# Four selective-scan layers: transfers in program order, delta's second half by transfer, softplus in one piece per chunk, another layout of the layer norm

## The chip, the cores and the metric

The kernel runs on one core of a Trainium2 chip. The metric is device time of one execution in microseconds (us), the median of several runs. A profile comes from one more execution, whose own time and span are given beside it. Engines are called as in the profile: PE (matrix multiplications; PEld its weight loads), DVE (vector), ACT (activation), POOL (GpSimd) and SP, which here only issues transfers (DMAs).

## What is computed

Eight images of 64 x 64 positions with 96 channels go through four layers one after the other, each `x = x + f(groupnorm(x))`. Cut to what matters, `f` is a projection, a depthwise convolution with SiLU, and selective scans over the 4096 positions for 192 channels of 16 states, in four directions (layers 0 to 2) or one (layer 3):

```python
x_dbl = einsum('bkdl,kcd->bkcl', xs, x_proj_w)          # xs: 4 orders of the positions
dts, Bs, Cs = split(x_dbl, [rank, rank + 16])
delta = softplus(einsum('bkrl,kdr->bkdl', dts, dt_proj_w) + dt_bias)
def step(h, inp):                                       # over the positions
    u_t, d_t, b_t, c_t = inp
    h = exp(d_t[..., None] * A) * h + (d_t * u_t)[..., None] * b_t[:, :, None, :]
    return h, einsum('bkdn,bkn->bkd', h, c_t)
y = sum of the directions + D * xs, put back in order
y = layernorm(y) * gamma + beta                         # over 192 channels; layers 0 to 2
return (y * silu(z)) @ out_proj_w.T
```

## The kernel before, in words

A hardware loop runs over the eight images; its body holds the four layers. All data is fp32.

*Chunks.* A layer walks through its directions in the order k = 0, 2, 1, 3, eight chunks of 512 positions each: 32 chunks for layers 0 to 2, 8 for layer 3, 104 per image. k = 0 and 1 run forward, k = 2 and 3 backward. The projection of a forward chunk (`project`, `keep_x_dbl`) gives the rows of its backward partner too; these go to memory (`xm`) and are read back later by `load_x_dbl`.

*Partitions.* 192 channels are three groups t of 64. A tile of 128 partitions holds one group for two states at a time (the halves of the partitions), so a chunk is 24 scans of 128 x 512 (`scan`, L872): 6 steps s (two halves of the states g, three groups t) of four.

*What a scan needs.* Its decay is `exp(delta * A)` from ACT (`decay`, L858), with delta's 64 channels in both halves of the partitions. Its input, delta times u times B, comes from PE in PSUM (`enter`, L841, tile dbu: 16 matmuls of 64 x 64 for two scans); they take `du_t` (positions on partitions) and diagonal matrices built from B (`diagonal` on POOL for the first half of the states, `diagonals` on ACT for the second). After four scans POOL multiplies by C (`read_out`, L890), and PE adds the states up (`add_up`, L904).

*How delta comes about.* PE turns x_dbl into positions on partitions and applies the weights (`turn_v`, L716: four blocks of 128 positions, which are every fourth one), ACT works out softplus in three steps (Abs, Exp, Ln), DVE finishes it (`delta_of`, L752), PE turns u (`turn_u`, L730) and DVE multiplies (`du_of`, L763), PE turns delta back (`turn_back`, L815) and ACT copies it out of PSUM (`keep_delta`, L820 and L824).

*Order.* Between `tc.manual_schedule` and `by_hand.close()` PE, DVE, ACT and POOL run in program order; SP's transfers are placed by the scheduler. Inside the scans the order is written out: a chunk has 24 slots, one per scan. At slot m an `enter` goes out for two scans ahead (even slots), the scan, a decay four scans ahead, an `add_up` (odd slots), and what `plan` holds for the slot, which prepares the next chunk. In the plan before, chunk i + 1 is prepared in two halves e of two blocks each: `turn_v` at slots 2, 3 and 9, 10, softplus at 4 to 6 and 11 to 13, `delta_of` at 8 and 16, `du_of` at 12 and 18, `turn_back` at 17, 18, 20, 21, `keep_delta` at 19, 20 and 23, `project` for the chunk after at 22 and 23, copied out at slot 1. `spread_c` loads C in two parts, each spread over the partitions.

*PSUM.* `ps_b` holds two tiles of two banks (dbu and the wide ones), `ps_y` two single banks, `ps_m` two single banks, which x_dbl, v, u_t, delta_ps and the convolution's sums use in turn.

*Ahead of the scans* stands the convolution (partly on PE, DVE, ACT with POOL), during which the layer's first chunk is prepared without the plan, and `by_columns` writes a transposed copy of u to memory. *Behind them*, in the scheduler's order, come layer norm and gate: for a pair of chunks PE centres y by matmuls with a centring matrix (ca for channels 0 to 127, two banks; cb for 128 to 191 of both chunks), ACT squares, PE averages over the channels into all 128 partitions (var, L535 and L537), ACT makes Ln and Exp, DVE multiplies (L542, L543).

Of the kernel before, what the change touches and what calls it, by code (L numbers as in the profile page):

```python
# [30 lines left out]
DI = 192  # L31
# [11 lines left out]
NEGMEAN, CEN_A, CEN_B, ONE, EPS, N_CONST = 416, 544, 672, 736, 737, 738  # L43
# [73 lines left out]
def kernel(ctx: ExitStack, tc: tile.TileContext, x_in, const_in, *rest):  # L117
# [3 lines left out]
    def pool(name, bufs, space=None):  # L121
# [19 lines left out]
        ps_m=pool("ps_m", 2, PSUM),  # L141
# [23 lines left out]
def layer(tc, env, x, x_of, x_to, n, ly):  # L165
# [5 lines left out]
    mean_w = const[:, MEAN : MEAN + 128]  # L171
# [3 lines left out]
    def mm(name):  # L175
        return env.ps_m.tile([128, CH], F32, tag="mm", name=name)
# [41 lines left out]
    by_hand.enter_context(tc.manual_schedule(engines={E.PE, E.DVE, E.Activation, E.Pool}))  # L218
# [3 lines left out]
    m_ps = mm("m_ps")  # L222
# [7 lines left out]
    v_ps = mm("v_ps")  # L230
    nc.tensor.matmul(v_ps[0:C, 0:1], groups, var, start=True, stop=True)
    scale = small.tile([C, 1], F32, name="scale")
    with tables(tc, "natural_log_exp_and_others"):
        nc.scalar.activation(scale, v_ps[0:C, 0:1], AF.Ln, bias=const[0:C, EPS : EPS + 1])
        nc.scalar.activation(scale, scale, AF.Exp, scale=-0.5)
        n_a = K * NT * NJ
        neg_a = env.wts.tile([128, 4 * NT * NJ], F32, tag="neg_a", name=f"neg_a{n}")[:, :n_a]
        nc.scalar.activation(neg_a, w[:, ly.a_log : ly.a_log + n_a], AF.Exp)
        nc.vector.tensor_scalar(neg_a, neg_a, -1.0, None, ALU.mult)
# [66 lines left out]
    def by_taps(half, both, first=0, end=ly.taps):  # L306

        d0, nd = widths[half]
        if first == 0:
            sums[half, both[0]] = mm("conv")  # L310
# [46 lines left out]
    def make_ys():  # L357
# [3 lines left out]
        tc, env, n, ly, w, u_mem, lambda half: u_chunk(half, 0), d, neg_a, make_ys, mm, wide  # L361
    )
    early = next(work)
    if not image:
        early_at = {2: early.project, 3: early.turn, 5: early.turn_back, 6: early.keep_delta}
        with tables(tc, "silu_and_others"):
# [9 lines left out]
        with tables(tc, "natural_log_exp_and_others"):  # L376
            early.softplus()
        with tables(tc, "silu_and_others"):
# [9 lines left out]
    else:  # L388
# [69 lines left out]
        with tables(tc, "silu_and_others"):  # L458
# [27 lines left out]
        with tables(tc, "natural_log_exp_and_others"):  # L486
            early.softplus(lambda: by_vector(0, 3, 0))
        with tables(tc, "silu_and_others"):
# [16 lines left out]
    with tables(tc, "natural_log_exp_and_others"):  # L505
        ys = next(work)
    by_hand.close()
    y_a, y_b = ys
    x = load_x(tc, env, x_of)
# [6 lines left out]
    if ly.norm:  # L516
        with tables(tc, "natural_log_exp_and_others"):
            neg, cen_a = const[:, NEGMEAN : NEGMEAN + 128], const[:, CEN_A : CEN_A + 128]
            cen_b = const[:, CEN_B : CEN_B + 64]
            for c in range(0, NCH, 2):  # L520
                pair = chunks[c : c + 2]
                ca, cb = wide("ca").rearrange("p (o l) -> p o l", o=2), mm("cb")
                for o, s in enumerate(pair):
                    nc.tensor.matmul(ca[:, o], cen_a, y_a[:, s], start=True, stop=False)  # L524
                    nc.tensor.matmul(ca[:, o], neg, y_b[:, s], start=False, stop=True)
                for first, weights, y in ((True, neg[:, 0:64], y_a), (False, cen_b, y_b)):
                    for s, at in zip(pair, halves):
                        nc.tensor.matmul(cb[at], weights, y[:, s], start=first, stop=not first)  # L528
                sq_b = piece("sq_b")
                nc.scalar.activation(sq_b, cb, AF.Square)  # L530
                var = [single(o, "var") for o in range(2)]
                for o in range(2):
                    sq_a = piece("sq_a")
                    nc.scalar.activation(sq_a, ca[:, o], AF.Square)
                    nc.tensor.matmul(var[o], mean_w, sq_a, start=True, stop=False)  # L535
                for o, at in enumerate(halves):
                    nc.tensor.matmul(var[o], mean_w[at], sq_b[at], start=False, stop=True)  # L537
                for o, (s, at) in enumerate(zip(pair, halves)):
                    rstd = piece("rstd")
                    nc.scalar.activation(rstd, var[o], AF.Ln, bias=const[:, EPS : EPS + 1])  # L540
                    nc.scalar.activation(rstd, rstd, AF.Exp, scale=-0.5)
                    nc.vector.tensor_tensor(y_a[:, s], ca[:, o], rstd, ALU.mult)  # L542
                    nc.vector.tensor_tensor(y_b[at, pair[0]], cb[at], rstd[at], ALU.mult)  # L543


    with tables(tc, "silu_and_others"):
        for c in range(0, NCH, 2):
            pair = chunks[c : c + 2]
            z_a, z_b = wide("z_a").rearrange("p (o l) -> p o l", o=2), mm("z_b")
# [11 lines left out]
            if not ly.norm:  # L561
                of_b = mm("whole")
# [37 lines left out]
def scans(tc, env, n, ly, w, u_mem, u_first, d, neg_a, make_ys, mm, wide):  # L600
# [13 lines left out]
    RS, SL = 6, 24  # L614

# [20 lines left out]
    banks = {}  # L636

    def bank(i, name, part=0):

        if i > 0:  # L640
            return mm(name)
        if part == 0:
            banks[name] = wide(name)
        return banks[name][:, part * CH : part * CH + CH]
# [14 lines left out]
    def project(i, half):  # L659
# [3 lines left out]
        if half == 0:  # L663
            dbls[i] = bank(i, "x_dbl")[0 : ly.x_rows]
# [5 lines left out]
    def keep_x_dbl(i):  # L670
# [7 lines left out]
        nc.scalar.activation(x_dbl, dbls[i], AF.Identity, bias=const[0 : ly.x_rows, ONE : ONE + 1])  # L678
        nc.sync.dma_start(c_mem[k][:, s], x_dbl[0:NS])
        if K > 1:  # L680
            nc.sync.dma_start(x_mem[k + 2][:, s], x_dbl[64 : 64 + XP])
        dbls[i] = x_dbl[0:XP]

    def load_x_dbl(i):
# [5 lines left out]
        x_dbl = small.tile([128, CH], F32, tag="x_dbl", name="x_dbl")[0:XP]  # L690
        nc.sync.dma_start(x_dbl, x_mem[k][:, c * CH : (c + 1) * CH])
        dbls[i] = x_dbl
# [14 lines left out]
    def turn_v(i, e, b):  # L707

        if e == 0 and b == 0:
            for name in ("delta_t", "du_t"):  # L710
                turned[i, name] = env.turned.tile([128, NB4, DI], F32, tag=name, name=name)
        if b == 0:
            v = bank(i, "v", e)[:, 0 : 2 * (DI + NS)]
            turned[i, e, "v"] = v.rearrange("p (b d) -> p b d", b=2)
        at = ly.dt_w + walk[i][0] * (DI + NS)
        nc.tensor.matmul(  # L716
            turned[i, e, "v"][:, b],
            block(2 * e + b, dbls[i]),
            w[0:XP, at : at + DI + NS],
            start=True,  # L720
            stop=True,
        )

    def turn_u(i, e, b):

        if b == 0:
            to = bank(i, "u_t", e)[:, 0 : 2 * DI]
            turned[i, e, "u"] = to.rearrange("p (b d) -> p b d", b=2)
        to, b_ = turned[i, e, "u"], 2 * e + b
        nc.tensor.transpose(to[:, b, 0:128], block(b_, u_of(i, 0)), ident)  # L730
        nc.tensor.transpose(to[:, b, 128:DI], block(b_, u_of(i, 1)), ident[0:64, 0:64])  # L731

    def softplus(i, e, part):

        v = turned[i, e, "v"]
        if part == 0:
            rests[i, e] = env.turned.tile([128, 2, DI], F32, tag="rest", name="rest")
            nc.scalar.activation(rests[i, e], v[:, :, 0:DI], AF.Abs)
        elif part == 1:
            nc.scalar.activation(rests[i, e], rests[i, e], AF.Exp, scale=-1.0)  # L740
        else:
            nc.scalar.activation(rests[i, e], rests[i, e], AF.Ln, bias=1.0)

    def keep_b(i, e):

        bt = small.tile([128, 2, NS], F32, tag="bt", name="bt", bufs=4)
        nc.scalar.copy(bt, turned[i, e, "v"][:, :, DI:])  # L747
        turned[i, e, "b"] = bt

    def delta_of(i, e):  # L750

        nc.vector.scalar_tensor_tensor(  # L752
            turned[i, "delta_t"][:, 2 * e : 2 * e + 2],
            turned[i, e, "v"][:, :, 0:DI],
            0.0,
            rests.pop((i, e)),
            ALU.max,
            ALU.add,
        )

    def du_of(i, e):
        here = slice(2 * e, 2 * e + 2)
        nc.vector.tensor_tensor(  # L763
            turned[i, "du_t"][:, here], turned[i, "delta_t"][:, here], turned[i, e, "u"], ALU.mult
        )

    def diagonal(i, b):


        if b == 0:  # L770
            diags[i, 0] = env.diags.tile([128, NB4, NH, 64, 2], F32, tag="diag", name="diag")
        of = turned[i, b // 2, "b"][:, b % 2, 0:NJ].rearrange("p (q j) -> p q j", j=2)
        nc.gpsimd.tensor_tensor(  # L773
            diags[i, 0][:, b],
            sel.unsqueeze(1).unsqueeze(3).to_broadcast([128, NH, 64, 2]),
            of.unsqueeze(2).to_broadcast([128, NH, 64, 2]),
# [3 lines left out]
    def diagonals(i, first, n_):  # L780

        if first == 0:
            diags[i, 1] = env.diags.tile([128, NB4, NH, 64, 2], F32, tag="diag", name="diag")
        for q in range(first, first + n_):
            b, q = divmod(q, NJ)
            nc.scalar.activation(  # L786
                diags[i, 1][:, b, q // 2, :, q % 2],
                sel,
                AF.Copy,
                scale=turned[i, b // 2, "b"][:, b % 2, NJ + q : NJ + q + 1],  # L790
            )

    def diagonals_of_first():

        diags[0, 1] = env.diags.tile([128, NB4, NH, 64, 2], F32, tag="diag", name="diag")
        for b in range(NB4):
            of = turned[0, b // 2, "v"][:, b % 2, DI + NJ :].rearrange("p (q j) -> p q j", j=2)
# [7 lines left out]
    def turn_back(i, o, part):  # L805


        if part == 0:
            deltas[i, "ps", o] = bank(i, "delta_ps", o)
        for b in (2 * part, 2 * part + 1):  # L810
            of = turned[i, "delta_t"][:, b]
            for half in range(o + 1):
                to = deltas[i, "ps", o][64 * half : 64 * half + 128 // (o + 1)]
# [3 lines left out]
    def keep_delta(i, t):  # L817
        delta = env.deltas.tile([128, CH], F32, tag="delta", name="delta")
        if t == 2:
            nc.scalar.copy(delta, deltas[i, "ps", 1])  # L820
        else:
            for half in range(2):
                of = deltas[i, "ps", 0][64 * t : 64 * t + 64]
# [89 lines left out]
    def close_sums(i, o):  # L913
# [24 lines left out]
        2: [(turn_v, 1, 0, 0)],  # L938
        3: [(turn_v, 1, 0, 1)],
        4: [(keep_b, 1, 0), (softplus, 1, 0, 0)],  # L940
        5: [(softplus, 1, 0, 1)],
        6: [(softplus, 1, 0, 2), (diagonal, 1, 0), (turn_u, 1, 0, 0), (spread_c, 1, 0)],
# [194 lines left out]
```

## Time and profile before

| what | us |
| --- | --- |
| median of 3 runs (31732.65 to 31753.77) | 31743.75 |
| the profiled execution, its time | 31703.4 |
| its span | 31698.6 |
| PE busy in it | 30814.0 (97%) |
| DVE busy | 28392.2 (90%) |
| POOL busy | 27178.5 (86%) |
| ACT busy | 26085.1 (82%) |

Busy time is the union of an engine's instructions. The ends of matmuls are modelled, so PE's share says that it had work queued rather than that it ran at its peak. A line of the profile names the line of the code, the engine, the operation and the tiles, out<-in, with the sizes; a matmul in fp32 shows as two MATMUL records, its two passes. Windows cut out of the span show which engine fills a stretch; a timeline shows each engine's instructions in order, with the idle time ahead of one and what ended it in brackets. The granted clock of PE is 1.00 in the scans, and 0.98 over the span.

### The profile page before, as it was taken

To read this page: it belongs to the slowest core of one execution; us is meant where nothing else is said; L and a number is where in the kernel's file an instruction comes from. 1 tells how busy PE (TensorE), PEld (TensorE's weight loads), DVE (VectorE), ACT (ScalarE), POOL (GpSimd) and SP (SyncE) were. 2 spreads that over 40 slices of the span, in tenths; PEclk is the share of its full clock that TensorE was granted. 3 is DMA by queue.
4 is the path that set the end of the run, shared out by engine and by line. 5 is a ranking of instruction groups with operands and counts; after the bars stand their busy time and mean duration, and the time that the engine had idled before them with its cause. 6 is when DMAs were issued, how large, how long until landed. Compare 5 with 4: busy or idle time off the path is not lost. (4 is left out here: it accounts for less than half of the span.)

```text
span 31698.6 us, 951914 instructions
## 1 busy us (share of the span) xinstructions
PE 30814.0 (97%) x402320; PEld 16776.3 (53%) x402320; DVE 28392.2 (90%) x29432; ACT 26085.1 (82%) x65064; POOL 27178.5 (86%) x9436
## 2 busy tenths in 40 slices
PE   9999999999999999999999999999999999999999
PEld 5555555555555545555455554555555555555555
DVE  9899898998989989899898998989989899898998
ACT  8788788887888878888788887878878888788887
POOL 8898788987889879898798987989878898788987
PEclk9999999999999999999999999999999999999999
DMA  3333233333333333333333333333323333333332
GB/s 90 78 76 85 72 90 79 75 86 73 89 80 74 87 72 88 80 74 87 73 88 80 74 87 74 87 79 74 87 72 89 80 74 86 72 90 79 75 86 72
DMA packets 1262156, 2544.89 MB, mean 80 GB/s; under 512 B 108560, under 2 KB 129296, under 8 KB 1234832
## 3 DMA queue, kind: packets, MB, share of 16 engines
q1 hardware_dynamic: 1257872, 2483.64, 33.3%
q8 instruction: 3192, 52.30, 0.7%
q14 instruction: 1092, 8.95, 0.1%
HBM read 2208.74 MB, written 274.46 MB: 78 GB/s over the span
## 5 line engine op out<-in xcount | busy, mean ns | idle before, releaser
L890 POOL TENSOR_TENSOR h<-h,c 128x2048 f32<-128x2048 f32 x4992 | 22723.0, 4557 | 1867.5 <-ACT state L886 625.9
L872 DVE TENSOR_TENSOR_SCAN h<-d_a,state,dbu 128x512 f32<-128x512 f32 x17472 | 21076.5, 1261 | 1130.2 <-PE dbu L841 687.9
L858 ACT ACTIVATE d_a<-delta,neg_a 128x512 f32<-128x512 f32 x19968 | 14166.5, 716 | 122.1 <-DVE h L872 101.3
L841 PE MATMUL dbu<-diag,du_t 64*64 64x128 f32 x319488 | 11142.2, 277 | 296.4 <-DVE h L872 224.7
L841 PEld LDWEIGHTS dbu<-diag,du_t 64*64 64x64 f32 x319488 | 8712.0, 133 | 5111.5 <-issue 4681.5
L904 PE MATMUL y_ps<-h,const 128*64 128x512 f32 x39936 | 10827.0, 617 | 119.1 <-POOL h L890 110.5
L786 ACT ACTIVATE diag<-const,bt 128x64 f32<-128x64 f32 x25600 | 7550.4, 344 | 14.0 <-PE dbu L841 7.8
L773 POOL TENSOR_TENSOR diag<-const,bt 128x512 f32<-128x512 f32 x3328 | 3475.2, 1045 | 335.0 <-ACT bt L747 246.3
L872 DVE TENSOR_TENSOR_SCAN h<-d_a,dbu 128x512 f32<-128x512 f32 x2496 | 2881.8, 1203 | 498.6 <-ACT d_a L858 216.2
L904 PEld LDWEIGHTS y_ps<-h,const 128*64 128x64 f32 x39936 | 2065.6, 135 | 1899.4 <-issue 1498.5
L716 PE MATMUL v<-w,x_dbl 39*128 39x208 f32 (+1 forms) x6656 | 2618.4, 477 | 8.3 <-DVE delta_t L752 7.3
L716 PEld LDWEIGHTS v<-w,x_dbl 39*128 39x128 f32 (+1 forms) x6656 | 1787.2, 317 | 1568.3 <-issue 883.1
L824 ACT COPY delta<-delta_ps 64x512 f32<-64x512 f32 x3328 | 1930.9, 580 | 566.7 <-PE delta_ps L815 519.6
L815 PEld LDWEIGHTS delta_ps<-const,delta_t 128*64 128x64 f32 (+1 forms) x19968 | 1637.0, 154 | 1415.7 <-issue 949.7
L815 PE MATMUL delta_ps<-const,delta_t 128*64 128x128 f32 (+1 forms) x19968 | 2223.8, 286 | 11.6 <-issue 11.6
L747 ACT COPY bt<-v 128x32 f32<-128x32 f32 x1664 | 300.8, 183 | 1848.7 <-PE v L716 1846.5
L730 PEld LDWEIGHTS u_t<-const,u 128*128 128x128 f32 x3328 | 650.1, 195 | 1583.2 <-issue 887.2
L886 ACT COPY state<-h 128x4 f32<-128x4 f32 x4992 | 972.4, 195 | 568.0 <-DVE h L872 527.9
L454 POOL TENSOR_TENSOR acc<-acc,more 128x512 f32<-128x512 f32 x576 | 756.7, 1317 | 699.6 <-ACT more L453 356.1
L730 PE MATMUL u_t<-const,u 128*128 128x128 f32 x3328 | 1292.2, 388 | 0.0
L320 PE MATMUL conv<-xn,taps 96*128 96x512 f32 (+1 forms) x2496 | 1160.0, 658 | 22.1 <-DVE taps L203 22.1
L731 PE MATMUL u_t<-const,u 64*128 64x64 f32 x3328 | 1098.8, 330 | 0.0
(99 smaller groups left out, 16194.5 us busy)
## 6 DMA issues: line engine op xcount, KB each, us to landing
c<-cm SPq DMA_DIRECT2D x1792, 512.0 KB
c<-xm SPq DMA_DIRECT2D x1536, 512.0 KB
u<-u SPq DMA_DIRECT2D x1088, 256.0 KB
u<-u SPq DMA_DIRECT2D x1088, 128.0 KB
u<-u SPq DMA_DIRECT2D x48, 1024.0 KB
x_mem<-x SPq DMA_DIRECT2D x48, 768.0 KB
x<-x_mem SPq DMA_DIRECT2D x48, 768.0 KB
x<-in_x_dram SPq DMA_DIRECT2D x32, 768.0 KB
```

Source lines behind the costliest of these rows:

```text
L320: nc.tensor.matmul(part, taps[:, t, d0 : d0 + nd], rhs, start=t == 0, stop=t == ly.taps - 1)
L716: nc.tensor.matmul(turned[i, e, "v"][:, b], block(2 * e + b, dbls[i]), w[0:XP, at : at + DI + NS], start=True, stop=True,)
L730: nc.tensor.transpose(to[:, b, 0:128], block(b_, u_of(i, 0)), ident)
L773: nc.gpsimd.tensor_tensor(diags[i, 0][:, b], sel.unsqueeze(1).unsqueeze(3).to_broadcast([128, NH, 64, 2]), of.unsqueeze(2).to_broadcast([1 ...
L786: nc.scalar.activation(diags[i, 1][:, b, q // 2, :, q % 2], sel, AF.Copy, scale=turned[i, b // 2, "b"][:, b % 2, NJ + q : NJ + q + 1],)
L815: nc.tensor.matmul(block(b, to), of_, ident, start=True, stop=True)
L824: nc.scalar.copy(delta[64 * half : 64 * half + 64], of)
L841: nc.tensor.matmul(to[64 * half : 64 * half + 64, e, b], du[rows, b, 64 * t : 64 * t + 64], diag[rows, b, 2 * half + pair], start=True, st ...
L858: nc.scalar.activation(d_a, deltas[i, t], AF.Exp, scale=neg_a[:, at : at + 1])
L872: nc.vector.tensor_tensor_scan(hs[s][:, m4, flow], decays.pop(m)[:, flow], p[:, flow], 0.0 if first else states[i // NCH][:, j : j + 1], A ...
L890: nc.gpsimd.tensor_tensor(hs[s], hs[s], cs[i, g], ALU.mult)
L904: nc.tensor.matmul(sums[i][o][64 * half : 64 * half + 64], sel, hs[of][:, state, :], start=g == 0 and e in (0, 4), stop=g == 1 and e in (3 ...
```

## The change

1. SP joins the engines in program order (`E.SP` in `manual_schedule`); the table loads on ACT are then written plainly.
2. `ps_m` becomes one tile of two banks. x_dbl, v, delta_ps and u_t each take it whole, one after the other; outside the scans its halves are used by turns.
3. `turn_v` makes two blocks per call as a pair: one from x_dbl on partitions 0 up, one from a second copy on partitions 64 up, which a transfer makes (`x_hi`, or a second load of xm). The weights stand on both halves of the partitions.
4. Softplus, `keep_b`, `delta_of` and `du_of` are one instruction each per chunk, of 768 elements (64 for `keep_b`) per partition.
5. `turn_back` writes each group once; `keep_delta` copies 64 partitions out by ACT and fills the other 64 by a transfer.
6. The upper half of POOL's fourth diagonal goes to ACT (36 instead of 32 there).
7. The plan is written anew for this, with `turn_back` ahead of `turn_u`.
8. Layer norm: the mean and cb share a tile of two banks, both chunks side by side on the halves of the partitions; DVE subtracts the mean in place, in 64-partition pieces; var is one bank for both chunks; one Ln and four Exp of 64 partitions; POOL multiplies y_a, DVE y_b.

The first chunk of a layer goes the old way in points 3 and 5, with both copies from ACT and no transfer. Cut to the core:

```diff
-    by_hand.enter_context(tc.manual_schedule(engines={E.PE, E.DVE, E.Activation, E.Pool}))
+    by_hand.enter_context(tc.manual_schedule(engines={E.PE, E.DVE, E.Activation, E.Pool, E.SP}))
...
-        ps_m=pool("ps_m", 2, PSUM),
+        ps_m=pool("ps_m", 1, PSUM),
...
+    def two_banks(name):
+        return env.ps_m.tile([128, 2 * CH], F32, tag="mm", name=name)
...
                 pair = list(zip(chunks[c : c + 2], halves))
+                mean, cb = wide("mean").rearrange("p (o l) -> o p l", o=2)
+                for p, work in (
+                    (mean, ((mean_w, y_a), (mean_w, y_b))),
+                    (cb, ((neg, y_a), (cen_b, y_b))),
+                ):
+                    for last, (weights, y) in enumerate(work):
+                        for s, at in pair:
+                            nc.tensor.matmul(p[at], weights, y[:, s], start=not last, stop=bool(last))
+                var = single(c // 2 % 2, "var")
+                for s, at in pair:
+                    for half in halves:
+                        nc.vector.tensor_tensor(y_a[half, s], y_a[half, s], mean[at], ALU.subtract)
+                    sq_a = piece("sq_a")
+                    nc.scalar.activation(sq_a, y_a[:, s], AF.Square)
+                    nc.tensor.matmul(var[at], mean_w, sq_a, start=True, stop=False)
...
+                ln = env.decays.tile([128, CH], F32, tag="d_a", name="ln")
+                nc.scalar.activation(ln, var, AF.Ln, bias=const[:, EPS : EPS + 1])
+                for s, at in pair:
+                    rstd = env.decays.tile([128, CH], F32, tag="d_a", name="rstd")
+                    for half in halves:
+                        nc.scalar.activation(rstd[half], ln[at], AF.Exp, scale=-0.5)
+                    nc.gpsimd.tensor_tensor(y_a[:, s], y_a[:, s], rstd, ALU.mult)
+                    nc.vector.tensor_tensor(y_b[at, pair[0][0]], cb[at], rstd[at], ALU.mult)
...
 def keep_x_dbl(i):
+        dbls[i] = [x_dbl[0:XP], x_dbl[0:XP]]
+        if i > 0:
+            there = small.tile([128, CH], F32, tag="x_hi", name="x_hi", bufs=1)[64 : 64 + XP]
+            nc.sync.dma_start(there, x_dbl[0:XP])
+            dbls[i][1] = there
...
+    def turn_v(i, b):
+        for e, of in enumerate(dbls[i]):
+            o = 64 if i > 0 and e else 0
+            nc.tensor.matmul(
+                turned[i, "v"][:, 2 * e + b],
+                block(2 * e + b, of),
+                w[o : o + XP, at : at + DI + NS],
...
 def keep_delta(i, t):
+        if i > 0:
+            here = halves[t % 2]
+            nc.scalar.copy(delta[here], deltas[i, "ps"][here, t // 2])
+            nc.sync.dma_start(delta[halves[1 - t % 2]], delta[here])
...
     plan = {
         0: [(load_u, 2)],
         1: [(keep_x_dbl, 1)],
+        3: [(turn_v, 1, 0)],
+        4: [(turn_v, 1, 1)],
+        5: [(keep_b, 1), (softplus, 1, 0), (spread_c, 1, 0)],
+        6: [(softplus, 1, 1), (diagonal, 1, 0)],
+        7: [(softplus, 1, 2)],
+        9: [(delta_of, 1)],
+        10: [(turn_back, 1, 0, 0), (diagonal, 1, 1), (close_sums, -1, 0)],
+        11: [(turn_back, 1, 0, 1)],
+        12: [(turn_back, 1, 1, 0), (keep_delta, 1, 0)],
+        13: [(turn_back, 1, 1, 1), (keep_delta, 1, 1), (diagonal, 1, 2)],
+        14: [(close_sums, -1, 1)],
+        15: [(turn_u, 1, 0, 0), (keep_delta, 1, 2)],
+        16: [(turn_u, 1, 0, 1), (spread_c, 1, 1)],
+        17: [(turn_u, 1, 1, 0), (diagonal, 1, 3)],
+        18: [(turn_u, 1, 1, 1)],
+        19: [(load_x_dbl, 2)],
+        20: [(du_of, 1)],
         22: [(project, 2, 0)],
+        23: [(project, 2, 1)],
     }
```

## The prediction, on record before the changed kernel ran

> **What bounds the kernel now.** The page first: PE 97% busy, DVE 90, POOL 86, ACT 82. Its chain of waits names PE, but the shares add up to 8% of the span, so it says who and not how much. So I went to the sums by window and cut one chunk of 512 positions out, from one `delta_of` to the next: first of a reversed direction (k = 2), then of a forward one (k = 1).
>
> ```profile
> core 0: us, PE busy (x) PEld busy (x) DVE busy (x) ACT busy (x) POOL busy (x), PEclk, DMA share, GB/s
> 503.67:535.55 31.88, 31.88 (x482) 18.40 (x477) 31.40 (x31) 28.86 (x77) 31.16 (x11) 1.00 0.39 80
> 691.79:725.76 33.97, 33.97 (x477) 18.96 (x477) 31.52 (x32) 29.66 (x77) 31.28 (x11) 1.00 0.31 80
> ```
>
> The period of a chunk is PE's busy time to 0.01 us, in both kinds: PE bounds, and the 2.08 us between the kinds are `project`, which only k < 2 needs. DVE has 0.48 us to spare in a reversed chunk and 2.45 us in a forward one, POOL 0.72 and 2.69, ACT about 3 and 4.3. So a saving on PE is worth its full size in a forward chunk, and in a reversed one only until DVE takes over. The timeline of PE then prices the pieces (starts subtracted; second column is to the modelled end, so a group costs the time to the next start).
>
> ```profile
> 505.43 0.71 PE L815 MATMUL delta_ps<-const,delta_t 128*128 128x128 f32 x4
> 506.07 1.10 PE L841 MATMUL dbu<-diag,du_t 64*64 64x128 f32 x32
> ...
> 509.79 0.66 PE L815 MATMUL delta_ps<-const,delta_t 128*64 128x128 f32 x8
> 510.28 1.03 PE L904 MATMUL y_ps<-h,const 128*64 128x512 f32 x4
> ...
> 516.79 0.80 PE L716 MATMUL v<-w,x_dbl 49*128 49x208 f32 x2
> 517.52 1.08 PE L904 MATMUL y_ps<-h,const 128*64 128x512 f32 x4
> ```
>
> A dbu takes 1.04, a y_ps 1.01, each of the four `turn_v` matmuls (two passes) 0.73, a full `turn_back` part 0.64, a half-width one 0.49 to 0.53. Groups follow each other without a gap.
>
> **The change, part by part.** *turn_v.* Its four matmuls become two pairs, one on rows 0 to 48, one on rows 64 to 112, into two banks. No line shows v like that, but the layer norm has such pairs:
>
> ```profile
> 1147.98 1.88 PE L535 MATMUL var<-sq_a,const 128*128 128x512 f32 x4
> 1149.79 1.13 PE L537 MATMUL var<-sq_b,const 64*128 64x512 f32 x4
> 1150.85 1.12 PE L524 MATMUL ca<-y,const 128*128 128x512 f32 x2
> ```
>
> Four passes on all rows take 1.81 us, four on two row halves into two banks 1.06, about what two passes alone take (0.97 for the L524 group). So a pair should cost what one cost: 0.75. Bounds: 0.73 (perfect) to 1.46 (no overlap). I take 0.75, the nearest row being the same shape of tile: 4 x 0.73 - 2 x 0.75 = 1.42 us off PE per chunk.
> *turn_back.* Eight matmuls instead of twelve, but the four dropped ran beside the others in the second column half (eight passes cost 0.51). Four passes without partner: between 0.25 (half of it) and 0.64 (the full-width part); I take 0.58, as (0.64 - 0.19 for the first weight load) / 4 = 0.11 a pass. That is 0.14 added per chunk. PE: 1.42 - 0.14 = 1.28 less, 30.6 and 32.7.
> *DVE.* A `delta_of` or `du_of` of 384 elements takes 0.45 start to start, a 512-wide sum 0.58, so 1.0 ns an element: 768 cost 0.85 against 2 x 0.45, and both save 0.1: 31.3 per chunk.
> *ACT.* Two 64x512 copies of 0.58 and part of a third go (1.06), softplus about 0.2, one `keep_b` 0.07; four more diagonals at 0.24 come: about 28.5. *POOL.* Half a diagonal less (1.00): 30.6. Neither bounds.
> *What is hidden.* The copies of delta by transfer: decided at slots 12, 13, 15, first read at slot 20, eight slots of 1.33 us after. A transfer takes 2.39 us from issue to landing here:
>
> ```profile
> 682.69 0.31 SPq L679 DMA_DIRECT2D cm<-x_dbl  x1
> 683.04 0.33 SPq L681 DMA_DIRECT2D xm<-x_dbl  x1
> 685.08 18.42 SPq L700 DMA_DIRECT2D c<-cm  x4
> ```
>
> (the read of cm waits for its write). 0.58 + 2.4 of 10.6: hidden, and without cover 2.4 us per chunk. In program order SP now stands at the three delta copies before it loads the second half of c; that is read 24 slots later. Five more issues of 0.3 us fall on a queue that mostly waits.
> *The new wait.* `x_hi` must land before the second matmul of `turn_v` at slot 3, and behind it in PE's queue stand the dbu that DVE scans next. In a forward chunk x_dbl's copy is ready at 682.6, so x_hi lands at 685.1; PE reaches slot 3's `turn_v`, by its order after two dbu and two y_ps (4.1 us) behind the end of `project`, some 0.5 us later. Cost 0; bounds 0 to 1 us. The single two-bank PSUM tile adds a wait of `turn_u` (slot 15) for ACT's last delta copy; ACT needs 1.2 us after scan 13 for it, PE 2.05 until it gets there. `turn_back` moved to slot 10 waits for `delta_of` at slot 9, 0.85 us against one dbu of 1.04. Both fit, by 0.2 us at the least.
> So a forward chunk goes to 32.7 (-1.27), bound by PE, and a reversed one to 31.44 (-0.45), bound by DVE with 0.1 us of wait. Each image has 104 chunks: 56 forward, 48 reversed; four forward ones are prepared ahead of the loop and gain nothing. 52 x 8 x 1.27 = 528, 48 x 8 x 0.45 = 173: 701 us.
> *First chunks.* There x_hi queues behind the transposed copies of u, with SP in program order:
>
> ```profile
> 1284.19 1.06 SPq L355 DMA_DIRECT2D u<-u  x2
> 1285.30 1.01 SPq L679 DMA_DIRECT2D cm<-x_dbl  x1
> ...
> 1292.99 12.44 SPq L700 DMA_DIRECT2D c<-cm  x4
> ```
>
> The write behind the 2 MB took 7.7 us. So PE stands at `turn_v` until about 1294, where it went through at 1287.67, and the scans, which waited anyway until 1291.49, go on at about 1295; part is made up. I take 2.5 us for the 24 first chunks of four-direction layers (bounds 0 and 6): 60 us lost.
> *Layer norm.* Today PE sets it: a pair of chunks every 8.47 us without a gap, 39 us a layer from the last sum. After, PE needs 1.94 + 1.94 + 2 x 1.0 = 5.9 per pair. But the chain of one pair grows: mean 1.94, four subtractions (DVE, 0.6 each), squares, var, Ln 0.7, four Exp of 0.6, products. In the built order PE's second half of pair 1's variance stands behind a matmul of pair 2's mean, which waits for pair 0's buffer, and DVE's subtractions of pair 1 stand behind pair 0's product. Going through with the rows' durations, the pairs end at 14, 21, 30 and 37 us. PE then stands still twice for about 3 us. What that does shows at the end of today's norm:
>
> ```profile
> 1179.83 3.75 PE L556 MATMUL z_a<-xc,w 96*128 96x512 f32 x4 [2.48 <-DVE y L542]
> 1183.37 3.32 PE L587 MATMUL out<-gate,w 128*96 128x512 f32 x4
> ...
> 1191.59 1.98 PE L556 MATMUL z_a<-xc,w 96*128 96x512 f32 x4
> ```
>
> After 2.48 us of idleness the same four matmuls take 3.75 instead of 1.98, and it lasts 6.8 us: 3 us lost each time. So 43 us against 39: 4 lost per layer; bounds -13 (two pairs in flight, no slow clock: 26) to +10. 24 layers: 96 us.
> The Trainium skill, "TensorE: Matmul & The Clock Gate", Part 1, says that the clock halves after an idle window of about 3.4 us and stays so for about 3.4 us of work. The row contradicts it, with 2.48 and 6.8. By the page neither gap surely throttles, the norm would take 37, and the whole sum would be about 144 us lower than mine.
>
> Sum: 701 - 60 - 96 = 545 us off the profiled execution (31703.4; its span 31698.6): 31158. The runs' median, 31743.75, lies 40 higher, so 31200.
>
> **The rivals.** (1) *The row halves don't overlap.* For it: v's weights are read with a step (317 ns a load against 190 for a plain 128-wide one) and may bound a pair; against: L537. Then only two of four group starts go, 0.19 each, and 0.24 is left after turn_back's 0.14: 0.24 x 800 = 190 gained, 156 lost, 31710: no change that can be told. (2) *x_hi is late in every forward chunk*, the slower side. For it: 0.5 us of margin, and SP in strict order; against: 2.39, seen in each chunk, with the queue empty then. The gain of 545 is gone at 1.31 us of wait in each of 416 chunks, a landing of 4.2 us instead of 2.4; at the 7.7 of the first chunks it would be 4.8 - 1.3 = 3.5 us x 416 over: 33200. (3) *The norm gets shorter*, 26 us: 24 x 17 = 408 less than forecast, 30790. For it: PE's 5.9 against 8.47; against: the order above. (4) *Three engines at 31 us a chunk disturb each other*: the reversed chunks keep 31.89 and the forward ones lose half: 528 / 2 - 156 = 108 gained, 31640.
>
> **How the numbers follow.** Forecast 0.55, (1) 0.10, (2) 0.10, (3) 0.15, (4) 0.10. The median's own spread is 21 us, 0.07%, so 0.2% (64 us) is what can be told. (1) counts half as the same, 0.04 as faster, 0.01 as slower; (2) is slower; of (4) 0.01 is the same, and the rest is faster: faster 0.83, same 0.06, slower 0.11. The forecast's own range is 31000 to 31400 (x_hi up to 0.3, norm 0 to +8, first chunks 0 to 6); with the nearer half of (3) below and (4) and (1) above it, 30830 to 31720, it leaves (2) out and half of (3).
>
> **What would show it.** Period of a forward chunk 32.7 with PE without a gap, of a reversed one 31.4 with DVE without a gap; v's pairs at 0.75; no wait of PE for x_hi but in first chunks; the norm at about 43 us. A forward chunk over 33 would break step one; a wait of PE for DMA in it, the margin; delta late at L858 of the next chunk, the cover.

## The result, and the profile after

The changed kernel takes 34138.3 us (median of 4 runs, 34117.6 to 34153.2) beside 31744.9 us for the kernel before: a ratio of 1.0754, 95% interval 1.0735 to 1.0772. It is 2393 us slower; 31200 was forecast. The profiled execution has a span of 34115.8 us, with a mean granted TensorE clock of 0.93 (0.98 before).

Windows over three chunks of the changed kernel, cut as in the prediction from one `delta_of` to the next: the first is of a reversed direction (k = 2), the second a forward one (k = 1), the third of the first direction (k = 0).

```profile
core 0: us, PE busy (x) PEld busy (x) DVE busy (x) ACT busy (x) POOL busy (x), PEclk, DMA share, GB/s
468.60:501.52 32.92, 30.81 (x468) 17.36 (x464) 31.31 (x29) 28.48 (x74) 30.86 (x11) 1.00 0.40 96
674.83:710.47 35.64, 34.18 (x472) 18.34 (x468) 30.74 (x30) 29.52 (x75) 30.87 (x11) 0.95 0.41 94
176.57:215.85 39.28, 36.85 (x472) 19.48 (x468) 31.81 (x30) 30.09 (x76) 30.75 (x11) 0.87 0.33 81
```

The busy times are those that were forecast: PE 30.8 where 30.6 was expected, DVE 31.3, ACT 28.5, POOL 30.9. But a chunk is now longer than any engine's work in it: in the first row PE stands idle for 2.11 us, and in the two others it also works at a lower clock. The groups say what it waits for (last columns: idle time just before the group, and what ended it):

```profile
L761 PE MATMUL u_t<-const,u 128*128 128x128 f32 x3328 | 1380.4, 415 | 1383.8 <-ACT delta L851 1383.8
L746 PE MATMUL v<-w,x_hi 39*128 39x208 f32 (+1 forms) x1664 | 677.9, 489 | 102.8 <-DMA x_hi<-x_dbl 102.8
L336 PE MATMUL by_turns<-xn,taps 96*128 96x512 f32 (+1 forms) x2496 | 1318.2, 739 | 243.6 <-ACT u L307 167.2 <-ACT u L314 44.1 <-DVE taps L213 32.3
```

1384 us of idleness stand before `turn_u`, released each time by ScalarE's copy of delta. One such wait, on PE's timeline of a reversed chunk:

```profile
442.65 1.10 PE L875 MATMUL dbu<-diag,du_t 64*64 64x128 f32 x32
443.69 1.08 PE L938 MATMUL y_ps<-h,const 128*64 128x512 f32 x4
446.22 0.39 PE L761 MATMUL u_t<-const,u 128*128 128x128 f32 x1 [1.45 <-ACT delta L851]
```

and ACT in the same microseconds:

```profile
441.44 0.58 ACT L851 COPY delta<-delta_ps 64x512 f32<-64x512 f32 x1 [1.01 <-PE delta_ps L844]
441.92 0.35 ACT L816 ACTIVATE diag<-const,bt 128x64 f32<-128x64 f32 x1
442.17 0.71 ACT L892 ACTIVATE d_a<-delta,neg_a 128x512 f32<-128x512 f32 x1
442.90 0.58 ACT L851 COPY delta<-delta_ps 64x512 f32<-64x512 f32 x1
443.51 0.35 ACT L816 ACTIVATE diag<-const,bt 128x64 f32<-128x64 f32 x1
443.76 0.71 ACT L892 ACTIVATE d_a<-delta,neg_a 128x512 f32<-128x512 f32 x1
444.38 0.58 ACT L816 ACTIVATE diag<-const,bt 128x64 f32<-128x64 f32 x2
444.85 0.71 ACT L892 ACTIVATE d_a<-delta,neg_a 128x512 f32<-128x512 f32 x1
445.58 0.58 ACT L851 COPY delta<-delta_ps 64x512 f32<-64x512 f32 x1
```

`turn_u` writes the tile that `keep_delta` reads, so it waits for the third copy. That copy ends a chain of 4.7 us in ACT's order (441.44 to 446.16): ahead of it stand two earlier copies, three decays and four diagonals. And the chain begins late: the first copy reads bank 0, whose transposes ended at 439.5, and yet waits 1.01 us for the transposes into bank 1 (L844, at 440.75 to 441.40). So the two banks of the tile count as one thing to wait for here.

In chunks with k = 0 an added copy of `close_sums` (0.58 us) lies in the chain and the wait is 2.2 us. What a wait of that size does next, on PE:

```profile
259.11 1.08 PE L938 MATMUL y_ps<-h,const 128*64 128x512 f32 x4
262.36 0.39 PE L761 MATMUL u_t<-const,u 128*128 128x128 f32 x1 [2.17 <-ACT delta L851]
...
264.60 1.97 PE L938 MATMUL y_ps<-h,const 128*64 128x512 f32 x4
...
267.23 1.98 PE L875 MATMUL dbu<-diag,du_t 64*64 64x128 f32 x32
```

The same four passes of y_ps take 1.97 instead of 1.08 us: the granted clock stands at 0.5 from 264.40 to 271.22. Summed over the records of the clock from the first scan to the last, PE spends 4676 us at half speed, 1287 before the change.

By stage: the scans, from the first to the last of each layer, grew from 27462 to 29191 us, and what lies between the layers and behind the last one from 4152 to 4834.

### The profile page after: what moved, and what is told of

Read it like the earlier page. It is cut to its first block, busy times and chain, and to the rows that moved or that the text cites. A ratio compares the mean times of both kernels' runs of the same rounds, so it can differ in the third digit from the quotient of the medians.

```text
span 34115.8 us, 942834 instructions
## 1 busy us (share of the span) xinstructions
PE 31072.7 (91%) x395920; PEld 16279.3 (48%) x395920; DVE 28641.8 (84%) x27960; ACT 26005.3 (76%) x63456; POOL 27117.0 (79%) x9628
## 5 line engine op out<-in xcount | busy, mean ns | idle before, releaser
L924 POOL TENSOR_TENSOR h<-h,c 128x2048 f32<-128x2048 f32 x4992 | 22717.3, 4551 | 4087.4 <-ACT state L920 1610.3
L875 PEld LDWEIGHTS dbu<-diag,du_t 64*64 64x64 f32 x319488 | 9112.7, 137 | 6024.6 <-issue 5411.9
L938 PE MATMUL y_ps<-h,const 128*64 128x512 f32 x39936 | 11417.4, 642 | 64.8 <-POOL h L924 64.1
L816 ACT ACTIVATE diag<-const,bt 128x64 f32<-128x64 f32 x28800 | 8384.1, 343 | 23.2
L800 POOL TENSOR_TENSOR diag<-const,bt 128x512 f32<-128x512 f32 (+1 forms) x3328 | 3130.1, 942 | 418.5 <-ACT bt L778 418.5
L844 PEld LDWEIGHTS delta_ps<-const,delta_t 128*128 128x128 f32 (+1 forms) x13568 | 1547.6, 162 | 1472.3 <-issue 913.8
L844 PE MATMUL delta_ps<-const,delta_t 128*128 128x128 f32 (+1 forms) x13568 | 2218.5, 290 | 0.0
L851 ACT COPY delta<-delta_ps 64x512 f32<-64x512 f32 x2400 | 1393.9, 581 | 848.3 <-PE delta_ps L844 809.3
L336 PE MATMUL by_turns<-xn,taps 96*128 96x512 f32 (+1 forms) x2496 | 1318.2, 739 | 243.6 <-ACT u L307 167.2
L746 PE MATMUL v<-w,x_dbl 39*128 39x208 f32 (+1 forms) x4992 | 1364.4, 478 | 1.3
L746 PEld LDWEIGHTS v<-w,x_dbl 39*128 39x128 f32 (+1 forms) x4992 | 932.0, 316 | 801.5 <-issue 467.9
```

The costliest lines, as they stand in the source:

```text
L336: nc.tensor.matmul(part, taps[:, t, d0 : d0 + nd], rhs, start=t == 0, stop=t == ly.taps - 1)
L746: nc.tensor.matmul(turned[i, "v"][:, 2 * e + b], block(2 * e + b, of), w[o : o + XP, at : at + DI + NS], start=True, stop=True,)
L800: nc.gpsimd.tensor_tensor(diags[i, 0][:, b, 0:n_], sel.unsqueeze(1).unsqueeze(3).to_broadcast([128, n_, 64, 2]), of.unsqueeze(2).to_broadc ...
L816: nc.scalar.activation(diags[i, g][:, b, q // 2, :, q % 2], sel, AF.Copy, scale=turned[i, "b"][:, b, g * NJ + q : g * NJ + q + 1],)
L844: nc.tensor.matmul(block(b, to), of_, ident, start=True, stop=True)
L851: nc.scalar.copy(delta[here], deltas[i, "ps"][here, t // 2])
```

## The experiments

Each ratio is to the kernel before, run beside it on the same chip; "+x us" is the difference of the two medians. The change itself stands at +2393.

**e1: turn_u later**

```diff
-        15: [(turn_u, 1, 0, 0), (keep_delta, 1, 2)],
-        16: [(turn_u, 1, 0, 1), (spread_c, 1, 1)],
-        17: [(turn_u, 1, 1, 0), (diagonal, 1, 3)],
-        18: [(turn_u, 1, 1, 1)],
+        15: [(keep_delta, 1, 2)],
+        16: [(spread_c, 1, 1)],
+        17: [(turn_u, 1, 0, 0), (turn_u, 1, 0, 1), (diagonal, 1, 3)],
+        18: [(turn_u, 1, 1, 0), (turn_u, 1, 1, 1)],
```

> The kernel after, with its four transposes of u moved from slots 15 to 18 into slots 17 and 18, two pairs each; du_of stays in slot 20. Theory (TensorE waits at turn_u for ScalarE's third copy of delta, 1.45 us in most chunks and 2.18 where k is 0, and the clock halves behind the wait): about 2.5 us of states and input matmuls now lie ahead of turn_u, so the wait goes and with it most of the slow clock; chunks with k of 2 and 3 fall from 34.0 to 31.5-32.0, with k of 0 from 37.4 to 33-34, with k of 1 from 35.0 to 33-34. Some 2.0-2.6 us in 800 chunks: 34138 -> 32000-32500 us. Rival (the transfers in program order, or ScalarE, VectorE and GpSimdE disturbing each other, set the chunk): the wait moves to another line and the time stays within 300 us of 34138.

Measured: 31975.2 us, 1.0081 (1.0064 to 1.0098), +250, just below the range. Windows over the same three kinds of chunk in this kernel:

```profile
429.43:460.56 31.13, 30.68 (x468) 17.34 (x464) 31.13 (x29) 28.38 (x74) 30.56 (x11) 1.00 0.47 102
621.67:654.43 32.76, 32.76 (x472) 17.84 (x468) 30.72 (x30) 29.09 (x75) 30.87 (x11) 1.00 0.43 104
170.33:203.62 33.29, 32.75 (x472) 17.91 (x468) 31.51 (x29) 29.63 (x76) 30.76 (x11) 1.00 0.38 97
```

The reversed chunk is DVE's busy time to 0.01 us, the forward one PE's. Moving three of the four calls of `turn_u` by one or two slots, with no work taken away, gave back 2143 of the 2393 us: the wait is the cause of these. The idle time ahead of `turn_u` went from 1384 us to nothing, and the time at half clock fell from 4676 to 2239 us. The scans together are at 27020 us, 442 less than before the change; outside them nothing moved (4841).

**e2: a shorter chain.** The same wait from ACT's side: five of its diagonals leave the chain.

```diff
-        *((9, 2), (10, 2), (11, 3), (12, 1), (13, 1), (14, 2), (15, 1), (16, 2), (17, 3), (18, 2)),
+        *((9, 2), (10, 2), (11, 3), (16, 2), (17, 3), (18, 2)),
...
+        *((28, 1), (29, 2), (30, 1), (31, 1)),
```

> The kernel after, with the five single diagonals that ScalarE makes in slots 12 to 15 put off to slots 28 to 31, turn_u where it was. Theory: four of them lie in ScalarE's chain between its first and its third copy of delta, 0.24 us each in line, so turn_u is let go about 1.0 us sooner: its wait falls from 1.45 to about 0.5 us, and from 2.18 to about 1.2 with k of 0, and shorter waits halve the clock less often: 0.8-1.6 us in 800 chunks, 34138 -> 32850-33500 us. Rival (the transfers or the engines' mutual disturbance set the chunk): within 200 us of 34138. A second rival (ScalarE starts late whatever it does, because its first copy waits for TensorE's transposes into the other bank): the wait falls by less than 0.5 us.

Measured: 32657.3 us, 1.0293 (1.0276 to 1.0311), +932, a little better than the range. The wait fell from 1.45 to 0.59 us (four diagonals at 0.22), with k = 0 from 2.18 to 1.33:

```profile
L761 PE MATMUL u_t<-const,u 128*128 128x128 f32 x3328 | 1309.7, 394 | 698.7 <-ACT delta L851 698.7
```

0.86 us less waiting brought 1.8 us a chunk (1461 / 800); with the wait, the time at half clock fell too, from 4676 to 2625 us.

**e3: the chain made longer.** Both halves of each delta by copies.

```diff
-            nc.scalar.copy(delta[here], deltas[i, "ps"][here, t // 2])
-            nc.sync.dma_start(delta[halves[1 - t % 2]], delta[here])
+            for half in halves:
+                nc.scalar.copy(delta[half], deltas[i, "ps"][here, t // 2])
```

> The kernel after, with both halves of each delta read out of PSUM by ScalarE, as before the change, and no transfer (three more copies of 64 rows a chunk, about 0.55 us each in line, and three fewer DMAs). Theory: two of the added copies lie ahead of the third readout, turn_u waits 1.0 us or more longer in each of 800 chunks, and ScalarE, at 26 us of 34, has room for the rest: 34138 -> 34900-35600 us. Rival (the three transfers, or SP's queue behind them, cost the time): 32500-33800 us.

Measured: 36631.0 us, 1.1549 (1.1530 to 1.1568), +4906: the direction and the wait (1.45 to 2.74 us) as expected, the size missed by 1000 us.

```profile
L761 PE MATMUL u_t<-const,u 128*128 128x128 f32 x3328 | 1476.1, 444 | 2416.0 <-ACT delta L852 2416.0
```

Two things were left out: PE waits 0.4 us more at the second half of `turn_back`, which writes bank 1 while ACT still reads bank 0, and the half clock, 7226 us of it instead of 4676.

**e4: the kernel before with the new layer norm.** Lines 518 to 543 of the kernel before replaced by those of the change.

> The kernel before with the changed kernel's layer norm alone. Theory: the stage's own chain is longer (39.8 -> 48.6 us from first to last instruction in each of 24 layers by the two traces), and the halved PSUM has little to do with that: 31745 -> 31850-31980 us. Rival (the norm is shorter as it moves work off VectorE, and only the shared PSUM tile makes it long): 31100-31700 us.

Measured: 31984.3 us, 1.0081 (1.0064 to 1.0098), +259, at the upper edge (the range ended 4 us lower). The stage ends 54.9 us after the layer's last scan where it ended at 46.6 (layer 0, mean of eight images). It is longer by itself. PE in that stage of the changed kernel, the rows before which it stood idle for over 2 us:

```profile
1227.27 2.26 PE L558 MATMUL var<-sq_a,const 128*64 128x512 f32 x3 [3.10 <-ACT sq_a L557]
...
1238.06 1.93 PE L547 MATMUL mean<-y,const 128*64 128x512 f32 x6 [2.76 <-DVE y L570]
...
1248.41 1.07 PE L558 MATMUL var<-sq_a,const 128*64 128x512 f32 x2 [2.75 <-ACT sq_a L557]
...
1258.42 2.08 PE L583 MATMUL z_a<-xc,w 96*128 96x512 f32 x2 [3.13 <-POOL xc L580]
```

Three stops of about 3 us inside the norm, where the kernel before had none, and one ahead of z, which was 2.48 us before.

**e5: the convolution in separate tiles**, on top of e1, in the layer with the one-dimensional convolution only.

```diff
-            sums[half, both[0]] = mm()
+    turn = cycle((0, 1))
...
+            sums[half, both[0]] = mm() if image else single(next(turn), "conv")
```

> The kernel of e1 (turn_u in slots 17 and 18, 31975 us against 31725 of the kernel before in the same call), and in the layer with the one-dimensional convolution (plain) each convolution group in a PSUM tile of its own (the two banks y0 and y1 in turn) instead of a half of one two-bank tile. Theory (a half counts as the whole tile, so TensorE's next group waits until ScalarE has read the one before, and the wait halves the clock): the stretch from the first xn to the next scan of that layer falls from 77 to 52-58 us, eight times: 150-200 us off, a ratio to the kernel before of 1.0015-1.0040. Rival (the stage is long because SP, ScalarE's table loads or the first chunk's chain are late in program order): less than 60 us off, 1.006 or more.

Measured: 31768.7 us, 1.0021 (1.0012 to 1.0031), +57, 193 less than e1. From the first normalised chunk to the layer's scans the change had made 77.2 us of 51.7; the stage is 24 us shorter now. The growth came about because the groups of the convolution take the halves of one tile in turn. PE in the changed kernel:

```profile
3858.57 5.39 PE L336 MATMUL by_turns<-xn,taps 96*64 96x512 f32 x12 [0.78 <-ACT u L307]
3865.45 5.49 PE L336 MATMUL by_turns<-xn,taps 96*128 96x512 f32 x6 [1.49 <-ACT u L307]
```

and in e5, where three groups (6 passes, 12 side by side as six pairs, 6 again) run in a row behind the first wait:

```profile
3620.50 12.73 PE L337 MATMUL conv<-xn,taps 96*128 96x512 f32 x24 [4.04 <-DVE taps L213]
...
3635.12 2.84 PE L337 MATMUL conv<-xn,taps 96*128 96x512 f32 x6
```

In the changed kernel a group waits until ACT has read the group before it out of the other half, as in the two rows. The granted clock is 0.50 there from 3848.39 to 3872.28, and six passes cost 5.49 us; at full clock, as in the last row, they cost 2.84.

**e6: the old layer norm back**, on top of e1, its cb in one half of the two-bank tile.

> The kernel of e1 with the old layer norm (128-row means, both rows' variance in two banks), its cb in a half of the two-bank tile. Theory (the new norm costs the same here as in the kernel before, where it took 259 us): 200-280 us off, a ratio to the kernel before of 0.9990-1.0020. Rival (the old norm needs the PSUM rotation that is gone, so that in this kernel the new one is as good): within 80 us of e1, 1.0055 or more.

Measured: 31959.4 us, 1.0076 (1.0059 to 1.0093), +248. A miss for the theory: nothing came back, and the norm ends at 56.0 us. The old norm needs two tiles for cb; in one it is as slow as the new one.

**e7: no x_hi for the second chunk of a layer**, on top of e1.

```diff
-        if i > 0:
+        if i > 1:
             there = small.tile([128, CH], F32, tag="x_hi", name="x_hi", bufs=1)[64 : 64 + XP]
...
-            o = 64 if i > 0 and e else 0
+            o = 64 if i > 1 and e else 0
```

> The kernel of e1, with the second chunk of each layer taking all of its x_dbl from rows 0 up, with no x_hi (as the first chunk does); from the third on as before. Theory (x_hi's transfer stands in SP's program order behind the layer's first loads and its late landing holds TensorE 1.2 to 5 us in each first chunk, 32 in all): those waits go and with them some slow clock: 80-180 us off, a ratio to the kernel before of 1.0025-1.0055. Rival (the first chunk is late anyway, by the loads of u and by VectorE's first scans): less than 50 us off, 1.0065 or more.

Measured: 31882.6 us, 1.0049 (1.0032 to 1.0066), +171: 79 less than e1, at the lower edge of the range. PE's 5.0 us at x_hi in the first chunk of layers 0 and 2 are gone, and that chunk goes from 35.3 to 31.8 us in layer 0.

**e8: e1, e5, e6 and e7 together**

> The kernel of e1 with the edits of e5, e6 and e7 together. Theory (four separate losses that add up): 31975 less 150-200, 200-280 and 80-180 us: 31315-31545 us, a ratio to the kernel before of 0.987-0.994: the transfers, the row halves and the single instructions for a chunk are then a gain. Rival (they overlap, or a further loss of the change is still hidden): 31650 us or more, 0.9975 or more.

Measured: 31683.5 us, 0.9989 (0.9980 to 0.9999), -28, in the rival's range: e6's edit added nothing here either, and the other two add up (193 and 79 off e1's +250 gives -22).

**e9: e8 with the norm's tiles exchanged.** cb, the last to be read, rotates over the two single banks; both variances go into the two-bank tile.

```diff
-                ca, cb = wide("ca").rearrange("p (o l) -> p o l", o=2), mm()
+                ca, cb = wide("ca").rearrange("p (o l) -> p o l", o=2), single(c // 2 % 2, "cb")
...
-                var = [single(o, "var") for o in range(2)]
+                var = two_banks("var").rearrange("p (o l) -> o p l", o=2)
```

> The kernel of e8 (31683 us against 31711 of the kernel before in its call: 0.9989) with its old layer norm laid out anew in PSUM: cb in the banks y0 and y1 in turn, both variances in the one two-bank tile. Theory (e6 gained nothing because cb, whose last reader ends the pair of chunks, was in the single tile, so that no two pairs overlap; the norm ended 56 us after the last scan in e6, 47 in the kernel before): the norm ends at 46-51 us, 5-10 us less in 24 layers: 120-240 us off e8, a ratio to the kernel before of 0.9910-0.9955. Rival (any one of the norm's products in a single tile holds it up alike, variances too): within 70 us of e8, 0.9970 or more.

Measured: 31400.0 us, 0.9898 (0.9881 to 0.9914), -327: 1% faster than the kernel before, and better than the range. The norm ends at 46.9 us (layer 0, as above), where the kernel before has 46.6. Which of the norm's products sits in the single tile decides 299 us.

**e10: SP's transfers in the scheduler's order**, on top of e1.

```diff
-    by_hand.enter_context(tc.manual_schedule(engines={E.PE, E.DVE, E.Activation, E.Pool, E.SP}))
+    by_hand.enter_context(tc.manual_schedule(engines={E.PE, E.DVE, E.Activation, E.Pool}))
```

> The kernel of e1 (31975 us, 1.0081) with SP's transfers in the scheduler's order again, all else as it is. Theory (the transfers' order is of no account in steady chunks, and costs 1 to 5 us in 32 first chunks at most): within 130 us of e1, a ratio to the kernel before of 1.004-1.010. Rival (program order holds up loads of u and of c, or the copies of delta, everywhere): 1.000 or less, or, where program order is what brings delta and x_hi in time, 1.015 or more.

Measured: 34570.0 us, 1.0893 (1.0875 to 1.0912), +2843. My theory fell; the rival's second half holds. The decays' row:

```profile
L892 ACT ACTIVATE d_a<-delta,neg_a 128x512 f32<-128x512 f32 x19968 | 13990.1, 713 | 3105.3 <-DMA delta<-delta 3073.3 <-DVE h L906 30.9
```

and SP's queue in one forward chunk of e10:

```profile
691.84 1.23 SPq L728 DMA_DIRECT2D c<-cm  x2
693.17 2.82 SPq L852 DMA_DIRECT2D delta<-delta  x3
```

beside one of e1:

```profile
627.92 4.62 SPq L852 DMA_DIRECT2D delta<-delta  x3
632.63 1.29 SPq L728 DMA_DIRECT2D c<-cm  x2
```

In this chunk the scheduler has put the two broadcasts of c (512 KB each) first; they wait for POOL to free a buffer (`c<-cm` waits 16289 us in all for the read-out L924), and the small copies of delta (128 KB) stand behind them in the queue. The last of these is issued by 695.99, and the decay that reads delta starts only at 701.98, after a wait of ACT of 4.25 us. That the copies also pass behind the broadcasts' bytes is likely, but their landing is not in the profile. x_hi comes late here as well: PE waits 555 us for it in all, 104 in e1.

```profile
L746 PE MATMUL v<-w,x_hi 39*128 39x208 f32 (+1 forms) x1664 | 756.5, 543 | 559.1 <-DMA x_hi<-x_dbl 555.3 <-DVE h L906 3.5
```

So the transfers of delta are hidden in the order of the program, and not in the scheduler's.

**e11: no row halves**, on top of e1: all four products of `turn_v` from rows 0 up; x_hi and the second load of x_dbl are left out too (not shown).

```diff
-            o = 64 if i > 0 and e else 0
+            o = 0
```

> The kernel of e1 without the row halves: all four products of turn_v take x_dbl from rows 0 up, one after the other; x_hi and the second load of x_dbl are gone. Theory (TensorE bounds the chunk once turn_u no longer waits, and the pairs take 1.42 us of its work out of each chunk): 800 chunks longer by 1.0-1.5 us, 31975 -> 32750-33200 us, a ratio to the kernel before of 1.032-1.047. Rival (VectorE's scans hold the chunk together, of which e1 shows 0.4-0.7 us a chunk before the input products, so TensorE's work is worth little): 1.009-1.020.

Measured: 32574.7 us, 1.0266 (1.0249 to 1.0283), +847: 597 more than e1, between the two ranges. PE bounds the forward chunk here too (33.67 us, PE busy 33.67), but it is 0.91 longer and not 1.4:

```profile
621.42 1.26 PE L746 MATMUL v<-w,x_dbl 49*128 49x208 f32 x4
622.62 1.10 PE L875 MATMUL dbu<-diag,du_t 64*64 64x128 f32 x32
```

Four passes in one group take 1.20 us start to start, where the kernel before had twice two passes at 0.73. So of the 1.42 us about 0.5 comes from having two groups instead of four (2 x (1.46 - 1.20)), and 0.9 from the row halves (2 x (1.20 - 0.74)).

**e12: e9 with delta by copies**, as in e3.

> The kernel of e9 (0.9898 of the kernel before) with both halves of each delta read out of PSUM by ScalarE and no transfers of delta, as in e3. Theory (e3 made turn_u wait 1.29 us longer by two added copies and the other bank's transposes; slots 17 and 18 give turn_u about 1 us to spare beyond the 1.45 us, 0.3 where k is 0): waits of 0.2-0.5 us come back, near 1.0 with k of 0, and some slow clock: 31400 -> 31650-32300 us, a ratio of 0.9975-1.018. Rival (the transfers save nothing, since ScalarE has room and they bind SP's queue): 0.985-0.9935.

Measured: 32973.7 us, 1.0394 (1.0376 to 1.0411), +1260. The direction is the theory's, the size not: waits of 0.71 us at `turn_u` (1.43 with k = 0) and again 0.4 at `turn_back`. With 1 us to spare, 1.29 + 0.4 was too much. Transfers are worth 1587 us here, by ACT's chain and not by ACT's busy time (27169 of 33003 us).

## Why the prediction was wrong

**The step that failed** is: "The single two-bank PSUM tile adds a wait of `turn_u` (slot 15) for ACT's last delta copy; ACT needs 1.2 us after scan 13 for it, PE 2.05 until it gets there. ... Both fit, by 0.2 us at the least." It named the right wait and priced it at nothing, from one link of the chain. ACT had all nine rows of the timeline above to go through, 4.7 us, after the transposes that start it, and it starts late, as a reader of bank 0 waits for writers of bank 1. Measured: PE waits 1.45 us in most chunks, 2.2 with k = 0, 1384 us in all, and with the slower clock behind it this cost 2143 us. e1, e2 and e3 moved the wait by three different means, and the time followed.

**Right:** PE sets the forward chunk and DVE the reversed one. Once `turn_u` no longer waits they take 32.76 and 31.13 us, where 32.7 and 31.44 were forecast. The row halves run together: forward chunks show starts 0.06 us apart and less, and a pair takes 0.74. `delta_of` and `du_of` take 0.85 each. `x_hi` costs steady chunks nothing as long as SP keeps the program's order. By their busy time ACT and POOL don't bound; it was the order of ACT's work that held PE.

**Right in kind, wrong in size.** The scans' gain: 442 us in e1, where 701 - 60 was forecast. The largest piece is layer 1, whose chunks with k = 0 went from 35.18 to 35.95 us instead of gaining 1.27: there PE waits 2.36 us a chunk for DVE's scans in e1 (0.52 in layer 0), and I had counted all forward chunks alike. DVE makes the sums of layer 1's serpentine order of positions in four pieces there, 1.85 us instead of 1.44; what makes up the rest of the wait is open. The first chunks: e7 gives 79 us, 60 were put in. The norm: 43 us a layer forecast, about 48.8 measured from its first matmul to its last product (two stops of PE were seen coming, there are three and the one ahead of z), and 259 us in e4 for the 96 in the sum. Before, the same stretch took 40.2 us, so it grew by 8.6, inside the bound of +10; the 259 us, 10.8 a layer with the longer stop ahead of z, lie just outside it.

**Left out:** the convolution in one tile (193 us, e5). I weighed the shared tile at one place only, and it has three users: delta and u_t, the convolution, the norm.

**Hidden, as said, but by what.** The prediction costed the transfers of delta at nothing, under cover of eight slots, and at 2.4 us a chunk without. e10 takes the cover away by putting two broadcasts ahead, at 3.2 us a chunk (2593 / 800), of which PE's waits for x_hi are a part. So the part of the change that puts SP in program order is what makes the other part free; I had read it as a risk.

**The clock.** In the changed kernel 292 of 702 idle stretches of 1.0 to 1.5 us at full clock are followed within 3.6 us by half clock, and 288 of 305 of 2 to 3 us; of 698 stretches at half clock 697 last a whole multiple of 3.41 us, and all 698 begin on one grid of 3.413 us, to 10 ns. I had priced this in the norm, from the row with 2.48 us, and not asked what it would add to a stop in each of 800 chunks. The Trainium skill ("TensorE: Matmul & The Clock Gate", Part 1) names an idle window of about 3.4 us, which these counts contradict, and a window that runs free of the work, which the multiples and the grid fit.

The rivals: that the row halves do not overlap, that x_hi is late in each forward chunk, and that three engines disturb each other are excluded by e1's windows and e11; a norm of 26 us by e4.

What stays open: whether the first copy of delta would start sooner if the two banks were two tiles was not tried, as the eight banks are all taken; that a half counts as the whole is seen in the waits and in e5. In e9 the stretches between the layers are still 168 us longer than before (4285 and 4117 us), and no run says by what.

## What to carry to other kernels

When several small tiles are joined into one so that one instruction can span them, list every reader and writer of the joined tile in program order: here the readers of one half waited for the writers of the other, and the writers for the readers, and the release time was that of the reading engine's whole queue up to the last read, not that of the read. Here a stop of 1.5 to 2 us on TensorE cost one and a half times to twice its length (2143 us for 1384 in e1, 1461 for 685 in e2), so first move the waiting instructions by a slot or two, which cost no work in e1, before judging the idea. A cheap transfer stays hidden only as long as nothing that itself waits stands ahead of it in its queue (e10).

## What was not expected of the hardware

The clock halves after idle stretches of 1 to 1.5 us in 42% of the cases in this kernel, and in 11 of 127 in the kernel before. The traces show one thing that tells them apart: where in the grid of 3.413 us the stretch begins. Of the 560 among the 702 that stand at `turn_u`, all 89 that begin 3.0 us or more after a grid point are followed by half clock, and none of the 71 that begin 1.5 to 1.75 us after one. No run shifted a wait by a part of the grid to test it. Four passes of 49 rows cost 1.20 us in one group and 1.46 in two: how passes are grouped is worth about half as much as pairing them on row halves (0.26 us a group against 0.46).
